# Taking turns in the dense stage, and an earlier second head in layer 0's first step

## The chip, the cores and the metric

The kernel runs on one core of a Trainium2 chip. The metric is the device time of one execution in microseconds (us). A comparison uses the median of several executions; the profile shows one execution more.

## The reference

The input `x` is a batch of 8 images, each 256 channels by 32 x 32 pixels, that is 1024 tokens of 256 values. Everything is float32.

```python
# layer 0: attention with 8 heads of 64, softmax over the queries (axis=1)
xt = x.reshape(B, C, S).transpose(0, 2, 1)
qkv = (xt @ w_qkv + b_qkv).reshape(B, S, N_HEADS, 3 * D_K)
q, k, v = jnp.split(qkv, 3, axis=-1)
attn = jnp.einsum('bihd,bjhd->bijh', q, k) * SCALE
attn = jax.nn.softmax(attn, axis=1)
res = jnp.einsum('bijh,bjhd->bihd', attn, v).reshape(B, S, N_HEADS * D_K)
res = res @ w_out + b_out + xt
# layer 1: attention without heads on the normalized tokens n = _ln_t(t)
t = t + softmax((n @ W.T) @ n.T) @ n
# then a mixture of 8 experts, two of them per token
logits = tokens @ router_w.T            # tokens = _ln_t(t)
combine = the two largest softmax values, made to add up to 1, else 0
for e in range(E):
    h = gelu(tokens @ w1[e] + b1[e])
    out = out + combine[:, e:e+1] * (h @ w2[e] + b2[e])
t = t + out                             # out starts as tokens
```

## The kernel before, in words

The outer loop runs over the 8 images. For each image there is layer 0 (`layer0`), the attention of layer 1 (`attend`), the norm and the router (`normed`, `gates`). For images 0 to 6 the tokens are scattered to DRAM by expert (`dispatch`), and the experts' products for all of them run together while image 7 is in its attention (`experts`). Image 7's own experts are not routed: `dense` computes all 8 experts for all its 1024 tokens and weighs them with the gates.

Products go to PSUM through two pools. `big` hands out three buffers of 128 x 1024, `acc` two of 128 x 512. The order of the instructions on each engine is not written out fully by hand: a scheduler places each instruction when its inputs and its buffer are due by its own reckoning. A `with tc.issue_after(x)` holds what is issued inside it behind the instruction x in that order. [...]

**Layer 0.** `steps` runs over the four pairs of heads and, in each, over eight blocks of 128 keys: 32 steps per image. One step is: scores of head 0 and head 1 against all 1024 queries, each in two halves of 512 (`score(at, h, n)`, line 549, tile `psc`); for each head the max of the first half (`first_max`, line 564) and of the second half joined to it (`second_max`, line 573, output `scrap`, on VectorE); the exponential with its sum (`soften`, line 590, ScalarE, tile `ex`); the reciprocal of the sums and the values divided by them (`divide`, lines 604 and 606, tile `vs`); and, two steps later (LAG), the weighted values added up (`gather_values`, line 626, tile `po`). The keys of a block are in two parts of 64, so each score product uses a quarter of the array: 64 rows (the head) by 64 columns (the part of keys). The loop issues head 1's second half one step late, beside the first half of the next step's head 0.

At the end of the first step (`at == 0`) stand two more things: `begun.rest()`, the last two of the image's eight value products (`pv`, line 432, added to the bias at line 454 on VectorE), and, from image 1 on, the first part of the routing of the image before (`share()`: tiles `plT`, `g_l`, `g_m`, `g_p`). After step (0, 3) `project_pair` makes the next pair's queries and keys (`pqk`, line 402).

**Dense stage.** For expert e and half n of the tokens, in 16 rounds, `hidden(e, n)` makes 512 tokens' hidden layer: 4 products of 512 columns into a `big` buffer (`pdh`, line 1607), then two gelus on ScalarE (tile `dh`, line 1616). `collect(e, n, hT)` makes the output: 8 products of 256 columns into two `acc` buffers (`pdy`, line 1630), each of which VectorE adds to `t` with its gate (line 1640). After that `others.tick` adds up a piece of one of the images 0 to 6: `total` plus the two experts' rows `ys` (line 1529), a transpose into `oT` (line 1551), four stores to `out_dram` and the loads of a later piece, which SP issues. There are five slots for such pieces and 14 pieces. The program calls `hidden` one round ahead of `collect`. Ahead of the second round's `collect` stands `biases`: eight transposes (`pg`), a copy by ScalarE (`gT`), eight products (`pb`, line 1596) and four additions.

Both functions, `layer0` and `dense`, and what calls them:

## Time and profile before

| what | value |
|---|---|
| median of 3 runs (lowest, highest) | 2287.5 us (2286.29, 2294.09) |
| the profiled execution's own time | 2285.63 us |
| its span, first to last instruction | 2283.8 us |
| busy TensorE, VectorE, ScalarE, GpSimd | 98%, 69%, 54%, 14% |
| granted TensorE clock, mean | 0.999 |
| all score products, line 549 | 576.9 us |
| all weighted values, line 626 | 572.0 us |
| layer 0's first score product, images 0, 1, 7 | at 26.77, 265.74, 1703.67 us |
| dense stage, first `hidden` product | at 2152.2 us |

The times in views of the trace are counted from the span's start. A float32 product shows as two passes, so a `psc` of two parts of keys in one half is four records. A line of the timeline gathers a run of like instructions; in brackets stands how long the engine had been idle before it, and what ended the wait. Matmul ends are modelled, about 0.2 us past the point at which the next can begin; the chain of waits shows starts without that overlap.

### The profile page before, as it was taken

What the parts mean: (1) busy time and instruction counts of PE and PEld (TensorE: products, weight loads), DVE (VectorE), ACT (ScalarE), POOL (GpSimd) and SP (SyncE); (2) the same over time, 40 slices, a digit from 0 to 9 for tenths busy, and PEclk for the clock granted to TensorE, in tenths of its full rate; (3) what the DMA queues carried; (4) which work ended last, traced back from release to release, by engine and by line L of the source; (5) the groups of instructions that cost most, each with busy time, mean ns of one, the idle gap of its engine ahead of it and who ended that gap; (6) DMA issues with size and microseconds to landing.
All of it is one profiled execution on the core that took longest, in us unless ns stands there. A gap on an engine that the chain in (4) does not pass through costs nothing.

```text
span 2283.8 us, 38057 instructions
## 1 busy us (share of the span) xinstructions
PE 2243.0 (98%) x13061; PEld 1211.9 (53%) x13061; DVE 1568.4 (69%) x3923; ACT 1233.7 (54%) x2221; POOL 316.5 (14%) x321
## 2 busy tenths in 40 slices
PE   9999999999999999999999999999999999999997
PEld 3345634563356335643555345534563368885665
DVE  5775678557865787577756776678557857655676
ACT  3664566356636564746564664566356645555511
POOL 1000012000300030002000120012000315552100
PEclk9999999999999999999999999999999999999999
DMA  8996201020102010201011000200041136662485
GB/s 283 355 357 187 52 15 43 4 60 8 50 1 46 19 52 6 39 26 45 13 21 44 27 31 13 52 15 25 5 90 50 52 70 148 147 144 55 125 292 135
DMA packets 278265, 182.82 MB, mean 80 GB/s; under 512 B 196676, under 2 KB 233335, under 8 KB 277048
## 3 DMA queue, kind: packets, MB, share of 16 engines
q1 hardware_dynamic: 264808, 150.08, 24.3%
q0 software_dynamic: 11632, 29.78, 3.7%
q8 instruction: 104, 1.70, 0.3%
q14 instruction: 89, 0.73, 0.1%
q10 hardware_dynamic: 1632, 0.52, 0.1%
HBM read 63.47 MB, written 106.61 MB: 74 GB/s over the span
## 4 chain that ended last, share of the span: by engine, by line
PE 77%; issue 8%; ACT 4%; DVE 4%; POOL 3%; SPq 2%; DMA 2%; POOLq 0%; DVEq 0%; ACTq 0%
PE po L626 19%; PE psc L549 19%; PE pqk L402 7%; PE py L940 7%; PE pr L731 4%; PE pv L432 4%; PE ps L834 3%; POOL y L1444 3%; PE pdh L1607 2%; PE px L771 2%; SPq L923 2%; PE pqk L380 2%; PE pdy L1630 2%; PE ps1z L834 2%; ACT aT L923 1%
## 5 line engine op out<-in xcount | busy, mean ns | idle before, releaser
L590 ACT ACTIVATE ex<-psc,nmax 128x1024 f32<-128x1024 f32 x512 | 570.5, 1115 | 296.7 <-DVE scrap L573 215.0
L549 PE MATMUL psc<-qk,qk 64*64 64x512 f32 x4096 | 576.9, 592 | 4.1 <-ACT ex L590 4.1
L626 PE MATMUL po<-ex,vs 64*64 64x512 f32 x4096 | 572.0, 591 | 1.9 <-DVE vs L606 0.8
L573 DVE TENSOR_SCALAR_CACHE_REDUCE scrap<-psc,nmax 128x512 f32<-128x512 f32 x512 | 384.5, 751 | 157.5 <-PE psc L549 129.8
L564 DVE TENSOR_REDUCE nmax<-psc 128x1 f32<-128x512 f32 x512 | 350.7, 685 | 9.3 <-PE psc L549 9.3
L549 PEld LDWEIGHTS psc<-qk,qk 64*64 64x64 f32 x4096 | 180.3, 132 | 279.9 <-ACT ex L590 132.0
L626 PEld LDWEIGHTS po<-ex,vs 64*64 64x64 f32 x4096 | 176.0, 132 | 274.8 <-issue 82.4
L1196 POOL DMA_INDIRECT rows<-n,d_at x112 | 109.2, 975 | 462.7 <-DVE nmax L564 424.5
L402 PE MATMUL pqk<-xT,wqkv 128*128 128x512 f32 x384 | 171.2, 599 | 0.0
L1444 POOL DMA_INDIRECT y<-yb,to x126 | 124.5, 988 | 209.6 <-DVE yb L1437 183.6
L367 ACT ACTIVATE qk<-pqk,b_qks 128x512 f32<-128x512 f32 x124 | 85.6, 690 | 88.8 <-PE pqk L402 79.7
L402 PEld LDWEIGHTS pqk<-xT,wqkv 128*128 128x128 f32 x384 | 71.0, 190 | 99.9 <-issue 77.4
L923 ACT COPY spare<-home 32x256 f32<-32x256 f32 x272 | 109.4, 402 | 17.4 <-DVE home L911 11.9
L432 PE MATMUL pv<-wqkv,xT 128*128 128x512 f32 x244 | 116.4, 600 | 1.0 <-DVE v L454 1.0
L1383 PE MATMUL ph<-xb,w_ring 128*128 128x256 f32 x488 | 115.2, 379 | 0.9 <-DVE xb L1372 0.9
L1188 POOL IOTA n<- 128x8 f32 x14 | 2.0, 145 | 820.3 <-PE py L940 820.3
L940 PE MATMUL py<-n,spare 128*128 128x256 f32 x512 | 114.9, 379 | 0.0
L731 PE MATMUL pr<-wo,res 128*128 128x256 f32 x512 | 111.9, 379 | 0.7 <-ACT res L645 0.7
L1412 PE MATMUL pe<-w_ring,hb 128*128 128x256 f32 x472 | 111.5, 379 | 0.0
L1395 ACT ACTIVATE hb<-ph,b1T 128x256 f32<-128x256 f32 x126 | 52.8, 471 | 108.1 <-PE ph L1383 103.6
L940 PEld LDWEIGHTS py<-n,spare 128*128 128x128 f32 x512 | 96.4, 190 | 20.2 <-issue 4.3
L731 PEld LDWEIGHTS pr<-wo,res 128*128 128x128 f32 x512 | 97.2, 190 | 17.8 <-ACT res L645 4.7
(265 smaller groups left out, 2839.7 us busy)
## 6 DMA issues: line engine op xcount, KB each, us to landing
rows<-zero SPq DMA_DIRECT2D x7, 8256.0 KB
xr<-rows SPq DMA_DIRECT2D x252, 64.0 KB
xs<-in_x_dram SPq DMA_DIRECT2D x64, 128.0 KB
ys<-y SPq DMA_DIRECT2D x16, 512.0 KB
spare<-home SPq DMA_DIRECT2D x240, 32.0 KB
out_dram<-oT SPq DMA_DIRECT2D x58, 128.0 KB
xT<-in_x_dram SPq DMA_DIRECT2D x7, 1024.0 KB
sums<-t SPq DMA_DIRECT2D x7, 1024.0 KB
```

Source lines behind the costliest of these rows:

```text
L402: mm = nc.tensor.matmul(pq[:, ts(n, 512)], wqkv[:, cc, t, ts(g, P)], xT[:, cc, ts(n, 512)], start=(cc == 0), stop=(cc == NCC - 1),)
L432: return nc.tensor.matmul(pv, self.xT[:, cc, ts(i, P)], wqkv[:, cc, 2, :], start=(cc == 0), stop=(cc == NCC - 1),)
L549: mm = nc.tensor.matmul(pss[at, h][ts(c, DK), ts(n, 512)], k[r, j * P + c * DK : j * P + (c + 1) * DK], q[r, ts(n, 512)], start=True, stop ...
L564: firsts[at, h] = nc.vector.tensor_reduce(nmax, pss[at, h][:, ts(0, 512)], AX.X, ALU.max, negate=True)
L573: seconds[h] = nc.vector.tensor_scalar(scrap, pss[at, h][:, ts(1, 512)], -1.0, nmaxes[at, h], ALU.mult, ALU.min, accum_out=nmax,)
L590: nc.scalar.activation(ex, pss.pop((at, h)), AF.Exp, bias=nmaxes.pop((at, h)), scale=1.0, accum_out=sums[at][:, h : h + 1],)
L626: mm = nc.tensor.matmul(po[n][ts(h, DK), :], vss[at][keys, h, :], exps[at, h][keys, ts(n, 512)], start=(j == 0 and turn == 0), stop=(j == ...
L731: nc.tensor.matmul(pr[:, :C], res[g][:, ts(i, P)], wo[:, g, :], start=(g == 0), stop=(g == NPAIR - 1))
L923: move(to[ts(k, SQ), a], since[ts(a, SQ), k])
L940: evicted["mixed"] = nc.tensor.matmul(py[:, :D], aT[m], n1[:, m, :], start=(m == 0), stop=(m == NT - 1))
L1383: last = nc.tensor.matmul(ph[:, ts(fc, BR)], wb[:, dc * FF + fc * P : dc * FF + (fc + 1) * P], xb[:, dc, :], start=(dc == 0), stop=(dc == ...
L1444: sent = nc.gpsimd.indirect_dma_start(out=group.ways[R * b + r][:, :], out_offset=bass.IndirectOffsetOnAxis(ap=to[:, r : r + 1], axis=0), ...
```

## The change

In layer 0, for `at == 0` only, the second half of head 1's scores, its max and its exponential are issued at the end of step 0, ahead of `begun.rest()` and `share()`, instead of at the beginning of step 1. In the dense stage, each `hidden` is held behind the last product of the `collect` before it, and each `collect`'s products behind the last product of the `hidden` issued ahead of it; the very last `collect` is held behind nothing.

```diff
@@ -666,7 +666,7 @@
             if at <= last:
                 with tc.issue_after(counted.ins) if counted else nullcontext():
                     score(at, 0, 0)
-            if 0 < at <= last + 1:
+            if 1 < at <= last + 1:
                 with tc.issue_after(counted.ins) if counted else nullcontext():
                     score(at - 1, 1, 1)
                 second_max(at - 1, 1)
@@ -693,6 +693,9 @@
             elif at == last + 1:
                 evicted["divided"] = divide(last)
             if at == 0:
+                score(0, 1, 1)
+                second_max(0, 1)
+                soften(0, 1)
                 begun.rest()
                 share()
             if at >= LAG:
@@ -1600,17 +1603,18 @@
                     t2[:, i : i + 2, :], t2[:, i : i + 2, :], pb.rearrange("p (j d) -> p j d", d=D)
                 )
 
-        def hidden(e, n):
+        def hidden(e, n, behind):
             ph = big(f"pdh_{e}_{n}")
-            for fc in range(NFC):
-                for dc in range(NCC):
-                    nc.tensor.matmul(
-                        ph[:, ts(fc, 512)],
-                        table[:, e, dc * FF + fc * P : dc * FF + (fc + 1) * P],
-                        nT[:, dc, ts(n, 512)],
-                        start=(dc == 0),
-                        stop=(dc == NCC - 1),
-                    )
+            with tc.issue_after(behind.ins) if behind else nullcontext():
+                for fc in range(NFC):
+                    for dc in range(NCC):
+                        mm = nc.tensor.matmul(
+                            ph[:, ts(fc, 512)],
+                            table[:, e, dc * FF + fc * P : dc * FF + (fc + 1) * P],
+                            nT[:, dc, ts(n, 512)],
+                            start=(dc == 0),
+                            stop=(dc == NCC - 1),
+                        )
             hT = two.tile([P, NFC, 512], F32, tag="qk0", name=f"dh_{e}_{n}")
             for fc in range(NFC):
                 nc.scalar.activation(
@@ -1620,20 +1624,21 @@
                     bias=b1T[:, e * NFC + fc : e * NFC + fc + 1],
                     scale=1.0,
                 )
-            return hT
-
-        def collect(e, n, hT):
+            return hT, mm
+
+        def collect(e, n, hT, behind):
             for i in range(0, NT // NH2, 2):
                 py = acc(f"pdy_{e}_{n}_{i}")
-                for j in range(2):
-                    for fc in range(NFC):
-                        nc.tensor.matmul(
-                            py[:, ts(j, D)],
-                            hT[:, fc, ts(i + j, P)],
-                            table[:, e, NCC * FF + fc * D : NCC * FF + (fc + 1) * D],
-                            start=(fc == 0),
-                            stop=(fc == NFC - 1),
-                        )
+                with tc.issue_after(behind.ins) if behind else nullcontext():
+                    for j in range(2):
+                        for fc in range(NFC):
+                            mm = nc.tensor.matmul(
+                                py[:, ts(j, D)],
+                                hT[:, fc, ts(i + j, P)],
+                                table[:, e, NCC * FF + fc * D : NCC * FF + (fc + 1) * D],
+                                start=(fc == 0),
+                                stop=(fc == NFC - 1),
+                            )
                 with tc.issue_after(others.last.ins) if others.last else nullcontext():
                     for j in range(2):
                         block = n * (NT // NH2) + i + j
@@ -1654,16 +1659,17 @@
             if (e, n) == (E - 1, 0):
                 with tc.issue_after(added.ins):
                     others.last = store(b, t2[:, ts(n, NB), :], n)
-
-        pending = None
+            return mm
+
+        pending = collected = None
         for at, (e, n) in enumerate((e, n) for e in range(E) for n in range(NH2)):
-            now = (e, n, hidden(e, n))
+            hT, mm = hidden(e, n, collected)
             if at == 2:
                 biases()
             if pending is not None:
-                collect(*pending)
-            pending = now
-        collect(*pending)
+                collected = collect(*pending, mm)
+            pending = e, n, hT
+        collect(*pending, None)
         assert others.stored == len(others.todo)
 
     begun = Begin(0, next_x)
```

## Prediction

> **What bounds the kernel now.** I read the chain of waits first, then the timeline of TensorE in the two places that the diff touches, then the waits and granted clock there. The page's chain:

> ```profile
> ## 4 chain that ended last, share of the span: by engine, by line
> PE 77%; issue 8%; ACT 4%; DVE 4%; POOL 3%; SPq 2%; DMA 2%; POOLq 0%; DVEq 0%; ACTq 0%
> ```

> TensorE carries 77%, so a gain is TensorE idle time taken out, and any TensorE work left uncovered is a loss. Now the dense stage, TensorE's timeline (start, length, line, count of passes, idle before it). Line 1607 is `hidden` (below H), line 1630 `collect` (C); a product of 512 or 256 columns shows two passes, so one H is x8 and one C is x16.

> ```profile
> 2202.92 3.60 PE L1607 MATMUL pdh<-n2T,table 128*128 128x512 f32 x8
> 2206.36 3.62 PE L1630 MATMUL pdy<-table,dh 128*128 128x256 f32 x16
> 2209.81 7.03 PE L1607 MATMUL pdh<-n2T,table 128*128 128x512 f32 x16
> 2216.68 3.62 PE L1630 MATMUL pdy<-table,dh 128*128 128x256 f32 x16
> 2220.13 7.89 PE L1607 MATMUL pdh<-n2T,table 128*128 128x512 f32 x18
> ...
> 2242.35 3.70 PE L1607 MATMUL pdh<-n2T,table 128*128 128x512 f32 x8 [1.42 <-ACT dh L1616]
> ...
> 2254.46 7.07 PE L1630 MATMUL pdy<-table,dh 128*128 128x256 f32 x32
> 2263.56 8.90 PE L1630 MATMUL pdy<-table,dh 128*128 128x256 f32 x32 [2.04 <-DVE t L1640]
> 2274.43 3.69 PE L1630 MATMUL pdy<-table,dh 128*128 128x256 f32 x16 [1.96 <-DVE t L1640]
> ```

> Until 2209.81 H and C alternate without a gap. Then H runs ahead (two at once, then two and a quarter); PSUM fills up, H waits for gelus, and at the end only Cs are left. A C takes 3.45 us, but VectorE owes 1.76 (four t additions) + 2.47 (total) + 1.25 (transpose) = 5.48 us for it, so TensorE waits and its clock falls:

> ```profile
> 2260.00:2270.00 10.00, 7.96 (x30) 6.26 (x29) 9.51 (x15) 2.23 (x4) 0.00 (x0) 0.83 0.33 77
> ```

> The columns are length, busy PE, PEld, DVE, ACT, POOL, then granted clock 0.83, DMA share, GB/s. VectorE is at 95%. Earlier in the stage the chain shows H's other use, as filler while ScalarE copies gT:

> ```profile
> 2167.18 0.87 PE pg L1590 x8
> 2168.06 1.72 PE pdh L1607 x4
> 2169.78 3.83 PE pb L1596 x16
> ```

> Layer 0's first step, chain for image 1 (first score product at 265.74):

> ```profile
> 267.67 3.65 PE pv L432 x8
> 271.31 0.02 issue
> 271.34 0.69 DVE v L454
> ...
> 272.67 0.70 DVE scrap L573 x2
> ...
> 273.45 1.22 ACT ex L590 x2
> 274.66 0.04 issue
> 274.71 1.08 PE psc L549 x6
> 275.79 0.86 PE po L626 x8
> ```

> The second head's max (scrap) comes only after both value products, so its exponential at 273.45 starts 2.4 us after the first head's has ended, and TensorE waits for it. The timeline gives the same offsets in every image within 0.06 us, this exponential at +7.67 to +7.73 (+7.45 in image 0).

> [...]heads 0 and 1 sit in different rows, and their first score products start within 0.033 us. [...]head 1's first half, fifth in order, starts at 265.76, head 0's second half, third in order, at 266.65. [...]here an idle 2.04 us was enough: half clock from 2263.63 to 2267.05 (3.41 us).

> **Dense stage, costs.** One H and one C take 6.88 us (H at 2203.09 to H at 2209.97 in the chain). In the built order of the changed kernel, H(k+1) and C(k) alternate to the end.
> - Between the start of H8 (2209.97) and of C15 (2274.43) lie 64.46 us, with eight H and eight C. In turns they take 8 x 6.88 = 55.04. Gain 9.42. It is made of stalls of 1.40, 1.40, 2.19 and 2.13 between last and next product, about 1.75 of half clock, and 0.5 of slow restarts.
> - H3 may no longer start before C1. Its four filler passes go behind C1: TensorE idles from 2168.06 to 2169.78, loss 1.72. Could idling halve the clock? The trace does not show this gap empty; bounds are 0 and 1.7 us (3.41 us at half). I take 0, since 2.13 us idle before 2274.43 left the clock whole. It can't gain.
> - VectorE in turns: 5.48 of 6.88 us per round. It keeps up, as in the rounds before 2209. ScalarE's two gelus (1.27) fit in a C. Loads of `total` and `ys`, five rounds ahead: by the DMA records one lands about 8.2 us after its issue at this pace (2209.7 to 2217.9) and is used some 20 us after that (five rounds less the 5.8 from an addition to the next issue: 28.6 from issue to use). Stores have two oT buffers, 13.8 us, and land in about 6.4.
> - End: the first store's transpose of image 7 (1.25) now ends 0.4 us after VectorE could begin the last additions; this is mostly regained in C15's second half. Loss 0.1.
> Net 9.42 - 1.72 - 0.1 = **7.6 us**.

> **Layer 0, costs per image** (from its first score product; before to after):
> - The second head's second half joins TensorE's stream ahead of the values. It runs beside head 0's second half in rows that are idle there (four passes at 266.65 to 267.51), so the values still start at +1.86. Cost 0 on that cover; without it 0.86.
> - Its max runs at +3.46 instead of +6.87, and its exponential directly behind the first head's, at +5.23 instead of +7.71, ending with its sum at +6.53. The value additions go back 0.25 us; plT needs the first one's buffer at +5.40, free at +4.82: no wait. The gates' g_p moves behind a max and an exponential; next use at +16.9, so hidden.
> - What is late next: the next step's first head. Its two halves now run one after the other in their rows, done at +6.83 and +7.69, so the max starts at +7.69 (was 8.35) and vs at +8.57 (was 9.23): 0.66 earlier.
> - The first value sums po start at +8.93; before, head 0's rows were busy with step 2's scores until +9.88: 0.95 earlier. Then step 3's scores wait for the exponential at +10.35 (was 11.03): 11.60 against 12.46, 0.86 earlier. The same reckoning puts the projection at +15.14 against 15.99.
> - The built order shows a new TensorE wait on its own plT at the second po. Not in the trace before; bounds 0 and 0.2 us, no gain possible. I take 0: plT is over 3 us earlier.
> - SP and POOL issue the same instructions in the same order; nothing is moved past them.
> I take 0.85 (0.66 to 0.95). Eight images: **6.8 us** (5.3 to 7.6). The rest of the image is TensorE's row, so it arrives shifted.

> **Sum.** 7.6 + 6.8 = 14.4. Against the profiled execution's own 2285.63 (span 2283.8 and 1.8 around it) this is 2271.2. The median shown, 2287.5, is 1.9 above that execution, so I predict 2273.1 for the median. Own range: gain 11.2 (layer 0 at 5.3, dense with a halved clock 5.9) to 15.4, so 2270.2 on the profiled time to 2276.3 on the median.

> **Rivals.**
> 1. Layer 0's gain is absorbed: the steps after the first are held by VectorE, whose two maxima of each kind and vs add up to 3.4 us, about the 3.44 of TensorE's step. For: VectorE has 0.2 us idle in a step. Against: VectorE's own chain starts 0.66 earlier too. Only dense remains: 2287.5 - 7.6 = 2279.9.
> 2. The dense stage does not gain: in turns, TensorE has one H as slack, and late additions would stop it. For: VectorE at 80% of a round. Against: the four gapless rounds before 2209. Only layer 0 remains: 2280.7. If neither part works, 2287.5.
> 3. Slower, by the DMA of the dense stage. Each round moves 2.1 MB; in 6.88 us that is 305 GB/s, and 2190 to 2220 shows 309 to 319 GB/s at a share of 0.96 to 0.99. Today's wide rounds relieve it (0.61 to 0.67 from 2220 to 2250). Should the queue grow, the total's addition waits for its load, the t additions stand behind it on VectorE, PSUM stays full, and in strict turns no H may go ahead. It decides only once landing takes over 28.6 us instead of 8.2. To be 0.3% slower it must eat 14.4 + 6.9 = 21.3 us, 3.6 in each of the six rounds still fed by late loads, giving 2294.4. Against it: the load issued at 2189.3 also took 8.2 us, so no queue grows.

> **How the numbers follow.** Forecast 0.78; rival 1 0.09; rival 2 0.07; neither part 0.03; rival 3 0.03. About 0.3%, 6.9 us, is what a measurement of this kernel can tell from no change. Rivals 1 and 2 lie at that edge (2280.6), half on each side: faster 0.86, same 0.11, slower 0.03. The range goes from 2269.0 (own low end, with a microsecond of run spread) to rival 1's 2280.0.

> **What would show it.** In the new profile: H and C alternating x8, x16 with 6.88 us per pair to the end, no wait of line 1630's products for t above 0.3 us, granted clock 1.00 to C15; a gap of 1.7 us before pb; last C beginning 7.7 us earlier within the stage. In layer 0: second exponential at +5.2, first po near +8.9, first projection near +15.1, and each image about 0.85 shorter. Wrong would be: projections still at +16.0; VectorE waiting for loads; a half clock at the pb gap; or the value products starting at +2.7.

## The result, and the profile after

The changed kernel takes **2277.31 us** (median of 6 executions, 2275.55 to 2280.71), the kernel before in the same comparison 2291.41 (2286.29 to 2294.09). The ratio is 0.9946, with a 95% interval of 0.9931 to 0.9960: by this ratio 12.4 us faster, by the medians 14.1, where 14.4 were forecast.

The profiled execution of before (2285.63 us) is one of its quick ones and that of the changed kernel (2280.71 us, span 2279.0) the slowest of its six, so the two traces differ by only 4.9 us, and what they show has to be taken stage by stage.

The chain of waits on the page of the changed kernel:

```profile
## 4 chain that ended last, share of the span: by engine, by line
PE 85%; issue 4%; ACT 4%; DVE 3%; SPq 2%; DMA 1%; POOL 0%; DVEq 0%; POOLq 0%; ACTq 0%
```

TensorE's share of the chain has gone from 77% to 85%, though its busy share is 98% in both. Now the timeline of TensorE in the dense stage (start, length, line, passes, and in brackets the idle time before and who ended it). Line 1611 is `hidden` (H), 1635 `collect` (C), 1599 the biases `pb`.

```profile
2159.33 3.87 PE L1635 MATMUL pdy<-table,dh 128*128 128x256 f32 x16 [1.72 <-ACT dh L1620]
...
2168.91 4.36 PE L1599 MATMUL pb<-b_rows,gT 8*128 8x256 f32 x16 [1.42 <-ACT gT L1595]
2173.20 6.59 PE L1635 MATMUL pdy<-table,dh 128*128 128x256 f32 x16
2179.63 3.60 PE L1611 MATMUL pdh<-n2T,table 128*128 128x512 f32 x8
2183.06 3.62 PE L1635 MATMUL pdy<-table,dh 128*128 128x256 f32 x16
...
2262.27 3.60 PE L1611 MATMUL pdh<-n2T,table 128*128 128x512 f32 x8
2265.70 7.07 PE L1635 MATMUL pdy<-table,dh 128*128 128x256 f32 x32
```

From 2179.63 on, H and C alternate every 6.88 or 6.89 us without a bracket: the stalls of 1.4 and 2 us at the end of the stage are gone. The price stands at the top. TensorE waits 1.42 us for `gT`, where four passes of H used to lie, and then C1 takes 6.59 us instead of 3.6. Two stretches say why (length, busy PE, PEld, DVE for VectorE, ACT for ScalarE, POOL, granted clock, DMA share, GB/s):

```profile
2170.00:2180.00 10.00, 10.00 (x30) 7.28 (x29) 3.79 (x7) 0.00 (x0) 0.00 (x0) 0.66 0.66 196
2190.00:2220.00 30.00, 30.00 (x109) 20.41 (x108) 23.23 (x31) 6.33 (x10) 0.00 (x0) 1.00 0.95 304
```

In the first stretch TensorE is busy all 10 us and has a clock of 0.66; later in the stage it is whole, at a DMA share of 0.95. The trace's record of the granted clock places the half clock from 2172.22 to 2179.05, and another from 2148.33 to 2151.74. The same columns for the stretches between its changes:

```profile
2148.33:2151.74 3.41, 3.41 (x12) 0.89 (x11) 1.40 (x4) 1.05 (x2) 1.43 (x2) 0.50 0.01 0
2151.74:2172.22 20.48, 17.35 (x62) 9.99 (x61) 15.20 (x35) 6.70 (x10) 5.46 (x5) 1.00 0.86 293
2172.22:2179.05 6.83, 6.83 (x17) 5.01 (x16) 2.02 (x4) 0.00 (x0) 0.00 (x0) 0.50 0.58 196
2179.05:2278.04 98.99, 93.72 (x332) 62.63 (x330) 74.62 (x100) 16.46 (x26) 0.00 (x0) 1.00 0.70 207
```

In the record they last 3.413, 20.480, 6.827 and 98.987 us, that is 1, 6, 2 and 29 times 3.413; in before a half clock of 3.413 us is followed by 13.653 at the whole one, 4 times that. Where a place below is counted in steps of 3.413 us from a change of the clock, the step is taken from these lengths; what decides on the clock, and when, the traces don't show. The earlier half clock is why C0 at 2159.33 waits 1.72 us for a late gelu: the four other profiles with a half clock there (e3, e4, e5, e8) have this wait, the rest don't. It lies in code that the change doesn't touch.

Layer 0, chain of waits for image 1 (start, length, what). Offsets such as +3.47 count from the first score product at 265.29:

```profile
265.36 1.89 PE psc L549 x16
267.25 3.63 PE pv L432 x8
...
273.01 0.76 DVE scrap L573 x2
...
273.88 0.30 DVE vs L606
...
274.23 1.09 PE po L626 x8
...
277.03 1.00 PE psc L549 x8
```

The exponential (`ex`) that TensorE waited for has left the chain; what remains is the next step's max (`scrap`) and division (`vs`), as the prediction named it.

The dense stage in stretches, in us, from the starts of products (H0 and C2 are the first `hidden` and the third `collect`):

| kernel | H0 to pg | pg to C2 | C2 to C7 | C7 to C15 | C15 to end | sum |
|---|---|---|---|---|---|---|
| before | 14.85 | 11.79 | 37.87 | 57.75 | 9.39 | 131.64 |
| changed | 18.56 | 16.60 | 34.43 | 51.66 | 9.80 | 131.06 |
| e1, layer 0's part alone | 14.85 | 11.79 | 37.87 | 57.75 | 9.47 | 131.72 |
| e2, dense part alone | 14.85 | 16.60 | 34.43 | 51.66 | 9.74 | 127.28 |
| e3, fourth H free | 18.57 | 15.11 | 34.43 | 51.66 | 9.75 | 129.53 |
| e4, pb over 128 rows | 18.56 | 13.26 | 34.43 | 51.66 | 9.78 | 127.70 |
| e5, early scores, late max | 19.81 | 14.91 | 34.43 | 51.66 | 10.05 | 130.87 |
| e6, one more head ahead | 14.85 | 18.11 | 34.43 | 51.66 | 9.75 | 128.79 |
| e7, before with light end | 14.84 | 13.47 | 37.87 | 51.85 | 10.42 | 128.45 |
| e8, e3 and e4 together | 18.23 | 11.59 | 34.43 | 51.66 | 9.78 | 125.69 |
| e9, e8 and a product ahead | 14.85 | 11.58 | 34.43 | 51.66 | 9.71 | 122.23 |
| e10, e8 again | 14.84 | 11.59 | 34.43 | 51.66 | 9.77 | 122.29 |

Every kernel in turns has 34.43 and 51.66; what half clocks cost them stands in the first two columns.

### The profile page after: what moved, and what is told of

It is laid out like the page before. It is cut to its first block, busy times and chain, and to the rows that moved or that the text cites. A ratio compares the mean times of both kernels' runs of the same rounds, so it can differ in the third digit from the quotient of the medians.

```text
span 2279.0 us, 38069 instructions
## 1 busy us (share of the span) xinstructions
PE 2239.6 (98%) x13061; PEld 1209.0 (53%) x13061; DVE 1567.8 (69%) x3923; ACT 1232.1 (54%) x2221; POOL 316.3 (14%) x321
## 4 chain that ended last, share of the span: by engine, by line
PE 85%; issue 4%; ACT 4%; DVE 3%; SPq 2%; DMA 1%; POOL 0%; DVEq 0%; POOLq 0%; ACTq 0%
PE po L626 20%; PE psc L549 20%; PE pqk L402 7%; PE py L943 6%; PE pr L734 5%; PE ph L1386 4%; PE pe L1415 4%; PE pv L432 4%; PE ps L837 3%; PE pdy L1635 2%; PE pdh L1611 2%; PE px L774 2%; PE pqk L380 2%; SPq L926 2%; PE ps1z L837 1%
## 5 line engine op out<-in xcount | busy, mean ns | idle before, releaser
L590 ACT ACTIVATE ex<-psc,nmax 128x1024 f32<-128x1024 f32 x512 | 570.0, 1114 | 295.1 <-DVE scrap L573 212.5
L626 PE MATMUL po<-ex,vs 64*64 64x512 f32 x4096 | 568.7, 591 | 5.3 <-DVE vs L606 4.3
L549 PE MATMUL psc<-qk,qk 64*64 64x512 f32 x4096 | 566.5, 592 | 0.9 <-ACT ex L590 0.8
L573 DVE TENSOR_SCALAR_CACHE_REDUCE scrap<-psc,nmax 128x512 f32<-128x512 f32 x512 | 384.3, 751 | 158.0 <-PE psc L549 129.7
L626 PEld LDWEIGHTS po<-ex,vs 64*64 64x64 f32 x4096 | 173.3, 132 | 282.8 <-DVE vs L606 87.3
L549 PEld LDWEIGHTS psc<-qk,qk 64*64 64x64 f32 x4096 | 178.6, 132 | 271.2 <-ACT ex L590 125.0
L432 PE MATMUL pv<-wqkv,xT 128*128 128x512 f32 x244 | 116.4, 600 | 1.0 <-DVE v L454 1.0
```

The source lines that it names most:

```text
L432: return nc.tensor.matmul(pv, self.xT[:, cc, ts(i, P)], wqkv[:, cc, 2, :], start=(cc == 0), stop=(cc == NCC - 1),)
L549: mm = nc.tensor.matmul(pss[at, h][ts(c, DK), ts(n, 512)], k[r, j * P + c * DK : j * P + (c + 1) * DK], q[r, ts(n, 512)], start=True, stop ...
L573: seconds[h] = nc.vector.tensor_scalar(scrap, pss[at, h][:, ts(1, 512)], -1.0, nmaxes[at, h], ALU.mult, ALU.min, accum_out=nmax,)
L590: nc.scalar.activation(ex, pss.pop((at, h)), AF.Exp, bias=nmaxes.pop((at, h)), scale=1.0, accum_out=sums[at][:, h : h + 1],)
L626: mm = nc.tensor.matmul(po[n][ts(h, DK), :], vss[at][keys, h, :], exps[at, h][keys, ts(n, 512)], start=(j == 0 and turn == 0), stop=(j == ...
```

## The experiments

**e1: layer 0's part alone.** The kernel before with this:

```diff
-            if 0 < at <= last + 1:
+            if 1 < at <= last + 1:
...
             if at == 0:
+                score(0, 1, 1)
+                second_max(0, 1)
+                soften(0, 1)
                 begun.rest()
```

> Only layer 0's half of the change, the dense stage as before. Theory: the profile of the changed kernel shows the first projection 0.64 to 0.74 us earlier in each image but one, so eight images give 4.6 to 5.7 us: ratio to before 0.9975 to 0.998, the same offsets in the trace (second exponential +5.2, po +8.9, projection +15.3), and the dense stage unchanged, with the stall at its end. Rival: the timed gain of the whole change (12.4 us) comes mostly from layer 0, because the profiled dense stage gained only 0.5 us: then about 0.995 here.

Measured: 2284.43 us against 2289.65, ratio 0.9979 (0.9971 to 0.9987), so 4.8 us by the ratio and 5.2 by the medians, as the theory had it. In its trace the first projections lie at the offsets of the changed kernel to 0.02 us in all eight images, and the dense stage is that of before.

**e2: dense part alone.** The changed kernel with those lines taken back.

> Only the dense half of the change, layer 0 as before. Theory: strict turns save 7.6 us of stalls, less what the clock costs in the early part of the stage, 1.7 to 5.1 us by the profile of the changed kernel[...]: 3 to 8 us in a run, ratio 0.9965 to 0.9985. Rival: the dense half gives nothing, as that one profile suggests (131.1 us against 131.6): 0.9995 to 1.0005.

Measured: 2281.72, ratio 0.9971 (0.9959 to 0.9983), so 6.6 us by the ratio and 7.9 by the medians, within the theory's 3 to 8. The two parts add up to 11.4 (13.2 by the medians), within the spread of the 12.4 (14.1) of both. The half clock behind `pb` is here too: it comes with the dense part.

**e3: the filler back.** The changed kernel with the fourth `hidden` released:

```diff
-            hT, mm = hidden(e, n, collected)
+            hT, mm = hidden(e, n, None if at == 3 else collected)
```

> The changed kernel with the fourth hidden (H3) not held behind the collect before it, so that two of its four products fill the gap ahead of pb again. Theory (the filler counts): TensorE's gap of 1.4 us ahead of pb goes, 1.7 us gained for certain; and the half clock after pb (6.8 us in the changed kernel's profile, cost 3.4) goes too: dense stage 3 to 5 us shorter than in the changed kernel, ratio to before about 0.993. Rival (the half clock has to do with pb's products of 8 rows, not with the gap): 1.7 us gained and the clock still falls to half within 3.5 us of pb[...]; ratio about 0.9945.

Measured: 2277.92, ratio 0.9941 (0.9926 to 0.9957), which can't be told from the changed kernel. It is the rival's case: the gap is filled (pg to C2 falls by 1.49), and yet the clock is halved behind `pb`:

```profile
2166.20 1.88 PE L1611 MATMUL pdh<-n2T,table 128*128 128x512 f32 x4
2168.01 5.06 PE L1599 MATMUL pb<-b_rows,gT 8*128 8x256 f32 x16
2173.00 5.88 PE L1635 MATMUL pdy<-table,dh 128*128 128x256 f32 x16
```

So it isn't the idle gap, or not it alone: `pb` ran without a pause ahead of the half clock, which lasted from 2170.59 to 2177.42. The 3.41 us before that, 2167.18 to 2170.59, held 0.83 us of H and 2.58 us of `pb`. What is odd about `pb` is `8*128`: its products have 8 rows.

**e4: the same products over 128 rows.** The changed kernel, with 120 rows of zeros added to both inputs of `pb`:

```diff
-        b2_rows = two.tile([E, D], F32, tag="hb", name="b2_rows")
-        nc.sync.dma_start(b2_rows, b2)
+        b2_rows = two.tile([P, D], F32, tag="hb", name="b2_rows")
+        nc.gpsimd.memset(b2_rows, 0.0)
+        nc.sync.dma_start(b2_rows[:E, :], b2)
...
+        gT = two.tile([P, S], F32, tag="tr", name=f"gT_{b}")
+        nc.gpsimd.memset(gT, 0.0)
...
-            gT = two.tile([E, S], F32, tag="tr", name=f"gT_{b}")
-            nc.scalar.copy(gT, pg[:E, :])
+            nc.scalar.copy(gT[:E, :], pg[:E, :])
```

> The changed kernel with pb's products over 128 rows, 120 of them zeros, instead of 8; the gap ahead of pb stays empty. Theory[...]: no half clock follows pb, C1 runs at 0.216 us a pass, and the stretch from the last pg to H4 is 3.4 us shorter than in the changed kernel's profile. Rival (the gap ahead of pb does it, or zero rows count as idle): half clock as before in the same place, no change in time against the changed kernel.

Measured: 2274.71, ratio 0.9937 (0.9923 to 0.9952). The trace, with the same 1.42 us of idle time ahead of `pb`:

```profile
2167.39 3.91 PE L1602 MATMUL pb<-b_rows,gT 128*128 128x256 f32 x16 [1.42 <-ACT gT L1598]
2171.21 3.72 PE L1638 MATMUL pdy<-table,dh 128*128 128x256 f32 x16
```

C1 takes 3.72 instead of 6.59, and no half clock follows. The timed ratio can't tell this kernel from the changed one (the intervals overlap); the trace can. In both kernels `pb` fills a step of 3.413 us from the clock's changes almost exactly (2168.81 to 2172.22 in the changed kernel, from 0.1 us after the step's start; 2167.53 to 2170.94 here). On TensorE the rows are all that differs, and the new ones are zeros. So in this pair the clock goes with the rows: behind 8-row `pb` it was 0.50 (2172.22 to 2179.05), behind `pb` over 128 rows 1.00 (2165.00 to 2175.00 here), though 120 of these hold zeros. TensorE's busy time does not tell the two apart: 1.42 us of idle time and then `pb` without a pause in both. How the rows come to matter isn't shown, and other numbers of rows or columns were not tried. In these profiles the rows are worth 16.60 - 13.26 = 3.34 us.

**e5: early scores, late max.** The changed kernel with head 1's max behind the last two value additions again:

```diff
                 score(0, 1, 1)
-                second_max(0, 1)
-                soften(0, 1)
-                begun.rest()
+                added = begun.rest()
                 share()
+                with tc.issue_after(added.ins):
+                    second_max(0, 1)
+                soften(0, 1)
```

(`begun.rest()` returns its last addition here.)

> The changed kernel, but in layer 0's first step head 1's max (and with it the exponential) is held behind the last two value additions again; only its score products stay ahead of the value products. My theory: layer 0's gain comes from VectorE's and ScalarE's order (max and exponential early), so this kernel loses it: the second exponential back at about +7.2 to +7.7 from the image's first score product, first value sums po at about +9.6, first projection at about +15.9, and per image 0 to 0.15 us left of the 0.57 us that the change brought; the span about 4 us above the changed kernel's. The rival: the gain comes from TensorE's order alone (head 1's scores run in rows that are idle there), then the projection stays at +15.25 and the images stay about 0.5 us shorter than before. Dense stage as in the changed kernel in both.

Measured (one execution, 2281.96): neither. The first projection of image 1 is at +15.56, between 15.99 before and 15.25 changed; over the eight images the projections come 3.11 us earlier in sum, of the changed kernel's 5.34. The chain has the exponential back in it (the 1.89 us are ScalarE standing ahead of it, while its max, begun at +6.37, is not done):

```profile
270.70 1.89 issue
...
272.67 1.21 ACT ex L591 x2
```

So some 58% of layer 0's gain at the projection is there with early scores alone, and the early max brings the other 42%. The first share isn't purely TensorE's: with its scores ready earlier, the max also passes two of the routing's VectorE steps (`g_m`, `g_p`) that it stood behind before. In image 0, whose first step has no routing, early scores alone bring 0.36 of 0.70.

**e6: one more head ahead.** The changed kernel with the second step's head 0 issued ahead of the value products as well:

```diff
                 soften(0, 1)
+                score(1, 0, 0)
+                first_max(1, 0)
+                score(1, 0, 1)
                 begun.rest()
```

(and not at its old place).

> The changed kernel, and in each image's first step the scores of the second step's head 0 (both halves, with the first half's max) are issued ahead of the last two value products too. My theory: after the change the steps that follow the first are held by VectorE and ScalarE (max, exponential, division for two heads take about as long as TensorE's step), and the value products must run at some time, so nothing more is gained: first projection at +15.25 give or take 0.3, each image within 0.3 us of the changed kernel's; the value additions come later and can cost up to 0.3. The rival: TensorE's order still sets the first steps, then the projection comes up to 0.6 to 1 us earlier, 5 to 8 us over eight images. Dense stage as in the changed kernel in both.

Measured (one execution, 2280.86): worse than either said. Image 1's projection is at +15.83, 0.58 later than in the changed kernel; of the 5.34 us over eight images 1.73 are left. Its chain:

```profile
269.40 2.15 ACT ex L590 x4
...
271.78 0.29 DVE vs L606
272.07 0.61 DVE v L454
...
272.73 0.44 PE plT L1039 x2
```

The value additions (`v`) now stand behind a division that waits for the exponentials: the first at +6.84 instead of +4.14. The routing's transposes `plT` want its PSUM buffer and begin at +7.58 instead of +5.43, with the scores behind them. Image 0, which has no routing in its first step, keeps 0.64 of its 0.70. So one more head ahead is too far here; places in between were not tried.

**e7: before, with a light end.** No product is moved; the additions of the last pieces to `total` are cut.

```diff
-                    added = nc.vector.tensor_add(total, total, self.slots[at][:, k])
+                    some = slice(0, 1 if self.added > 10 else NB)
+                    part = total[:, some, : 8 if self.added > 10 else D]
+                    added = nc.vector.tensor_add(
+                        part, part, self.slots[at][:, k, some, : 8 if self.added > 10 else D]
+                    )
```

> The kernel before, but the additions to total of pieces 10 to 13 are cut to 8 values of each of the 128 partitions, so these pieces of the output lack the two experts' rows; VectorE thereby has about 2 us less to do in each of the last rounds, and nothing moves on TensorE. My theory on where the dense stage's 9.5 us came from: the two stalls of 2.19 and 2.13 us for the t additions and the 1.75 us of half clock come from VectorE being owed 5.48 us for a product of 3.45 and go here (about 6 us, with some of the 0.5 of restarts), while the two stalls of 1.4 us for gelus stay, since they come from the order of the products: start of the eighth hidden product to the last collect's (57.75 us before, 51.66 after) at about 51.5 to 54.5, two waits of 1.4 for the gelu in it, none above 0.5 for t. Rival: the stalls are TensorE's order (all hidden products early) whoever adds, through the PSUM buffers; then the stretch stays at 57 us or more.

Measured (one execution, 2282.22): C7 to C15 falls from 57.75 to 51.85, with this timeline:

```profile
2243.92 3.70 PE L1611 MATMUL pdh<-n2T,table 128*128 128x512 f32 x8 [1.42 <-ACT dh L1620]
...
2252.49 3.70 PE L1611 MATMUL pdh<-n2T,table 128*128 128x512 f32 x8 [1.42 <-ACT dh L1620]
2256.03 17.76 PE L1634 MATMUL pdy<-table,dh 128*128 128x256 f32 x80
```

Both waits for gelus stay, both for t are gone, and five Cs run as one. So about 5.9 of the 9.5 us were VectorE's debt in the last rounds, the rest the gelus. The change wins both without taking work from VectorE: with an H between two Cs, VectorE has 6.88 us for the 5.3 that it is busy in a round (5.27 and 5.28 in two rounds of the changed kernel). A by-product: e7's early part is that of the kernel before, and still it has a half clock behind `pb`, from 2174.39 (C1 takes 5.41 us, before 3.72; pg to C2 13.47, before 11.79). The kernel before can meet it too.

**e8, e9, e10: the two repairs together.** e8 and e10 are e3 and e4 in one kernel. e9 adds a product without use ahead of the dense stage, against the early half clock:

```diff
+        if norm is not None:
+            warm = big("warm")
+            for _ in range(1):
+                nc.tensor.matmul(warm[:, :512], ident, wqkv[:, 0, 0, :], start=True, stop=True)
```

> The changed kernel with both repairs of the gap ahead of the gates' biases: the fourth hidden product may run ahead of the second collect again, and the gates' bias products pb run over 128 rows, 120 of them zeros. My theory: the repairs add up; no half clock after pb, and hidden product to the pb products 14.85 us, from there to the end of the second collect's round 11.8 to 12, whole dense stage 124 us against 131.06 (changed) and 131.64 (before) when the early half-clock window costs nothing, 127.7 where it does. Median 2272 to 2275, 3 to 5 us below the changed kernel. The rival: with the filler back, pb's wait is covered anyway and the rows make no difference or the wide pb costs more than it brings; then the median is 2276 to 2278, as with the filler alone.

> The kernel of e8 with one product more (128 x 512, identity by a weight tile, into a PSUM buffer that nobody reads) ahead of the last two transposes before the dense stage, where TensorE waits 0.87 us for the last normalized block. My theory: the half clock at the beginning of the dense stage (2145.88 to 2149.29 in e8's profile, where hidden product to pg took 18.23 us instead of 14.85) comes from the 0.87 and 1.21 us of idle TensorE[...]; the product fills the first of them and costs nothing or 0.1 us, so hidden product to pg is 14.85 in its profile, the dense stage 122.3 us, and the median 1 to 3 us below e8's[...]. The rival: the 1.21 us that stay, with products of 32 columns behind them, are enough; then the half clock comes as before, stretch about 18.2, and the median is e8's or 0.1 to 0.9 us above.

> The kernel of e8 again, to stand beside e9 on the same chip. Theory and rival of e9 expect e8's number here: 2272 to 2275 median. In its profile, hidden product to pg is 14.85 or about 18.2 us[...]; from pg to the second collect's end 11.6 to 12 in both cases if zeros in unused rows keep the clock up.

Measured: e8 2274.03 (ratio 0.9925, 0.9909 to 0.9941); e10 2271.45 (0.9923, 0.9907 to 0.9938); e9 2270.64 (0.9919, 0.9904 to 0.9935). In the stage the repairs add up: pg to C2 falls by 1.49 in e3, 3.34 in e4 and 5.01 in e8 and e10. The timed ratios of e3, e4 and e8 overlap. e10's median lies 0.55 below the 2272 to 2275 that were expected. From e10's trace, TensorE's timeline, with nothing in brackets:

```profile
2164.10 3.80 PE L1602 MATMUL pb<-b_rows,gT 128*128 128x256 f32 x16
2167.82 3.72 PE L1638 MATMUL pdy<-table,dh 128*128 128x256 f32 x16
```

No gap and no half clock; the stage takes 122.29 us, 9.35 less than before. As in e4, the clock stays whole behind 128-row `pb`: C takes 3.72 us, and the 3.41 us from 2164.98 to 2168.40 (counted back in steps of 3.413 from the change of the clock at 2267.38) hold 2.83 us of `pb` and 0.58 of C. e9 is inconclusive: its profile has no early half clock, but neither has e10's without the product, and the medians differ by 0.8 us. Of the other profiles, 5 have the early half clock (changed, e3, e4, e5, e8) and 6 don't (before, e1, e2, e6, e7, e10). All five carry both parts of the change, none of the four with one part or neither has it; these are too few to say whether the change makes it likelier. It costs 3.4 to 3.7 us (H0 to pg 18.23 to 18.57 against 14.85); e5's 19.81 holds a second half clock.

## Why the prediction was right, and where its steps were off

The forecast's case held: both parts gain, faster, 2277.31 inside 2269.0 to 2280.0 and 4.2 above the point. That the total came so close is in part luck: layer 0 was put too high and a half clock at nothing, and a kernel before that was slower than reckoned made up for it. (The own range's upper gain, 15.4, doesn't follow from its terms: 7.6 and 7.6 make 15.2.) By steps:

- **Turns, 9.42 us: held.** C2 to C15 fell from 95.62 to 86.09, by 9.53. e7 confirms what it is made of: stalls for `t` with the half clock behind them (0.83 from 2260 to 2270 in before, 1.00 from 2250 to 2270 in e7), and stalls for gelus.
- **H3's filler, 1.72 us: held** as to idle time: with the clock whole (e4) pg to C2 is 13.26 against 11.79, 1.47. From the first `pg`, `pb` begins after 2.45 us instead of 2.69: `gT` is there before the filler used to end.
- **Clock at the pb gap, taken as 0 with 1.7 as the upper bound: failed.** The prediction had named a half clock at the pb gap as a sign of being wrong, and it came. It cost 3.34 us in the profile, and all four profiles of kernels in turns with both the gap and the 8-row `pb` (changed, e2, e5, e6) have it, at 1.65 to 4.85 us over e4's 13.26. The step's reason was that 2.13 us of idle time had once left the clock whole, so it asked only whether the gap would halve the clock. The gap is followed by 3.9 us of 8-row products, behind which the clock was halved in e3 and e7 without a gap; together they are 5.3 us. Why no profile escapes is my estimate, from the record's 3.413 us and these lengths: however the 5.3 us fall on two steps of 3.413, one holds at least 2.7 of them, and e7 has a half clock behind a step with 2.44 us of `pb` and 0.97 of C. In the kernel before, `pb` alone is 3.83 us, 1.9 in each step at the mildest: before and e1 escape, e7 doesn't. That what lies in one step sets the clock of the next isn't shown. The cost exceeds the bound, reckoned with 3.41 us, because the half clock lasted 6.83. Its first 3.41 us still held 0.98 us of `pb`; in e5, where they held 0.11, the clock was whole again after them.
- **End, 0.1 us: mis-sized.** C15 to the end is 9.80 against 9.39, 0.4.
- **Dense sum, 7.6 us: right with the clock whole.** Adding up the undisturbed stretches: 14.85 + 13.26 + 86.09 + 9.78 = 123.98, 7.66 less than before. The two half clocks of this profile take it to 131.06.
- **Layer 0, mechanism: held.** For image 1 predicted and measured: max +3.46, +3.47; second exponential +5.23, +5.21; values +1.86, +1.89 (the scores ran under cover); next max +7.69, +7.72; vs +8.57, +8.59; po +8.93, +8.94. `plT` made no wait.
- **Layer 0, size, 0.85 per image: mis-sized.** The first projection came at +15.25 for +15.14, 0.74 earlier, since a later block of scores waits for the exponential that frees its buffer and takes 1.00 us instead of 0.86 (277.03 in the chain). Over eight images that is 5.34 us at the first projection, with 0.40 in image 5. Then about 0.30 goes in image 3 and 0.45 in image 5, and in this pair of profiles 4.56 arrive at the first `hidden` product, counted from the first score product of image 0, not 6.8 (5.3 to 7.6). "It arrives shifted" was true, to about 0.1 us, in six images of eight.
- **Median against profiled execution, +1.9: mis-sized, and it covered the above.** Over the 49 executions of the kernel before that the experiments gave, the median is 2289.65, 4.0 above that execution. It loses more to half clocks in most of its other executions: those with a mean clock of 0.999 average 2285.07, those at 0.996 average 2293.03. Where in the program they lose it isn't shown, since only one was profiled. Thus 12.4 timed us stand beside 4.56 + 7.66 = 12.2 of undisturbed stretches; that half clocks cost both kernels about the same is my reading, not measured.

The rivals: the first (layer 0's gain absorbed) falls with e1, the second (dense gains nothing) with e2. The third (late loads) falls with the waits of VectorE from 2185 to 2272 (total, times, longest):

```profile
DVE t L1645 <- PE pdy L1635: 19.1, 26, 0.9
```

It waits for TensorE only. By the DMA records a piece's loads take at most about 8 us from first packet to last landing, about 9 to 9.5 from the issue (2213.97 to 2223.5), where the prediction reckoned with 8.2 from the issue and with trouble from 28.6; stores take at most 5.0 from first packet to last landing.

## What to carry to other kernels

Where one engine is owed more per product than the product lasts, keep the products that feed it apart by others: strict turns moved 9.5 us here without taking an instruction out. When a filler is taken away, ask not only how long the gap is but what runs behind it; behind `pb` over 8 rows the clock was halved in six profiles of eight here, with a gap ahead of it or without, behind `pb` over 128 rows in none of four, and the padding with zeros cost nothing in its time (3.72 us from the first `pb` to the next product with 128 rows in e10, 3.83 with 8 in the kernel before). And a single profile can lie several us from the median, as here 4.0 below (2285.63 for 2289.65) and 3.4 above (2280.71 for 2277.31): compare stage by stage.

## What was not expected of the hardware

```profile
2160.32 5.55 PE L1637 MATMUL pdy<-table,dh 128*128 128x256 f32 x16 [1.89 <-ACT dh L1622]
```

In before, the 3.41 us from 2171.47 to 2174.89 (26 steps of 3.413 ahead of the half clock at 2263.63) held 2.06 us of 8-row `pb` and 1.36 of C1, which begins at 2173.53, and none followed. In this pair 8-row products and idle time differ, and a share of work that is always enough can't be read off these traces.

- Losses of about 0.3 us stay with their place in the program: image 3 between second and third projection, and image 5 in its first steps and ahead of `px`, in the changed kernel, e1, e3, e4, e8, e9 and e10, mostly to 0.02 us. Where they come from stays open.
- Image 7's attention part varies between executions in code that nobody changed: its first `px` comes at +369.58, 368.44 and 369.26 in the kernels with layer 0 as before (before, e2, e7), and at +367.43 to 368.97 in seven with the changed one. So a single profile's span tells little below 1.5 us.
